# A selective scan on one core: where its decays, its step sizes and its carried state are issued

## The chip, the cores and the metric

The kernel runs on one core of a Trainium2 chip. The metric is the device time of one execution in microseconds. A run gives one such time; the kernel before was timed in three runs, and one further execution was recorded by the profiler.

## What is computed

The program is a network of four layers, each an attention-like part and a feed-forward part with a layer norm behind each, on x of shape (2, 1024, 1024) in float32. The change touches one part alone, the selective scan of the third layer. Cut to what matters, with batch b, channel d of 2048, state n of 16 and time l of 1024 (written here as 1024 steps for each of two sequences):

```python
dt = softplus(einsum('blr,dr->bdl', dt_r, dt_proj_w) + dt_bias)
A = -exp(A_log)                                  # (2048, 16)
def step(h, inp):
    x_t, dt_t, B_t, C_t = inp
    dA  = exp(dt_t[..., None] * A)               # decay
    dBx = dt_t[..., None] * B_t[:, None, :] * x_t[..., None]
    h = dA * h + dBx                             # state, (batch, 2048, 16)
    y = einsum('bdn,bn->bd', h, C_t)
    return h, y
y = (ys + D_param * xc) * silu(z)
out = einsum('bdl,hd->blh', y, out_proj_w)
```

Every other layer is as before.

## The kernel before

The two sequences are worked one after the other (b = 0, 1), and within a sequence the 1024 steps are two halves of 512 (u = 0, 1). In a half, the 2048 channels are 16 chunks (c) of 128, and a chunk is eight **slots**. Slot k of a sequence (0 to 255, the second half from 128 on) handles 16 channels with their 16 states: two tiles (m = 0, 1) of 128 rows, a row being one channel and one state, by 512 steps.

For a slot, `rows` (line 1269) loads dt*x of the slot's channels from DRAM (`dxd`), copied to all 16 states, into a tile h; `times_b` (1278) multiplies it by B on GpSimd; `decay` (1283) spreads dt over the rows with a matmul into PSUM (line 1286) and takes Exp of it times A on ScalarE (1288); `scan` (1293) runs the recurrence on VectorE with one instruction over the 512 steps (1296), decay from PSUM, dt*x*B from h; `times_c` (1306) multiplies by C on VectorE; `states` (1311) sums over the states with matmuls (1318) into y's PSUM tile, every second slot. The tile h has nine buffers.

In the first half a scan starts from 0.0, and `keep` (1300) copies the last column of h to `hst` on ScalarE. In the second half `decay` has one operation more (line 1291): on ScalarE it adds decay times the kept state to the first column of h, and the scan again starts from 0.0.

The step size dt of a chunk comes from `l2_dt` (1208), called 16 slots before the chunk's first slot. It issues a matmul and hangs a chain of small operations of 128x512 on later slots: ScalarE's Relu, Abs, Exp (`act1`), add one, Ln, subtract one (`act2`), then GpSimd's sums (`pool1`, `sum1`), the product with x (`times_x`, 1237, followed by four DMAs that write dxd), and the split of dt into two parts for the decay's matmul (`parts` on ScalarE, `rest` on GpSimd, `send` with two DMAs). x itself is loaded into `xi` by a DMA. The tiles e, one, lg and rl of the chain have one buffer each, and `y_out` (1328) takes the tile "one" as well: it copies y out of PSUM on ScalarE, multiplies by silu(z) on GpSimd and writes it to DRAM.

The order is written out by hand in one loop over k (1479 to 1529). Each engine runs its instructions in the order in which this loop issues them, and waits for semaphores of the others. `at(k, f)` puts f into the list `late[k]`; these run in the middle of slot k, between its two scans. A slot also issues two matmuls (three ahead of slot -1) of other work, taken from a list `todo`: the z projection and the second half's x projection, or the output projection of the first half; their results are copied, convolved or passed through Silu by further `late` operations. All PSUM tiles come from one pool of 8 banks. All DMAs named here go through SyncE's queue (SP), in order.

Of the kernel before, what the change touches and what calls it, by code (L numbers as in the profile page):

```python
# [11 lines left out]
AF = mybir.ActivationFunctionType  # L12
ALU = mybir.AluOpType
# [14 lines left out]
class Net:  # L28
# [1032 lines left out]
    def l2_attn(self, b, ready, last):  # L1061
        nc, i = self.nc, self.i
        NCH, N, NR = 16, 16, 64
        NF = NR + 2 * N
        SL = 8 * NCH
        with (
# [24 lines left out]
            hst = lp.tile([P, NCH * N], F, name=self.nm("hst"))  # L1091

            def tmp(tag, bufs=2, n=HALF):
                return tp.tile([P, n], F, tag=tag, bufs=bufs, name=self.nm(tag))
# [4 lines left out]
            xcd, yd = [dram(t, [P, HALF]) for t in ("xcd", "yd")]  # L1099
# [3 lines left out]
            px, norms, hl, hs, dA, py, xs = {}, {}, {}, {}, {}, {}, {}  # L1103
# [6 lines left out]
            def at(k, f, *args):  # L1110
                late.setdefault(k, []).append((f, args))
# [96 lines left out]
            def l2_dt(u, c, k):  # L1208

                p = self.ps()  # L1210
                nc.tensor.matmul(
                    p, wd[c // 8][: NF + 1, (c % 8) * P : (c % 8 + 1) * P], norms[u][0], start=True, stop=True
                )
                xs[u, c] = xc = tmp("xi")
                at(k + 3, nc.sync.dma_start, xc, xcd[u][c][:])
                e, one, lg = tmp("e", 1), tmp("one", 1), tmp("lg", 1)
                dt, dtx = lg, e
                rl = tmp("rl", 1)

                def act1():  # L1220
                    nc.scalar.activation(rl, p, AF.Relu)
                    nc.scalar.activation(e, p, AF.Abs)
                    nc.scalar.activation(e, e, AF.Exp, scale=-1.0)

                def act2():
                    nc.scalar.activation(one, e, AF.Identity, bias=self.one)
                    nc.scalar.activation(lg, one, AF.Ln)
                    nc.scalar.activation(one, one, AF.Identity, bias=neg)

                def pool1():  # L1230
                    nc.gpsimd.tensor_tensor(e, e, one, ALU.subtract)
                    nc.gpsimd.tensor_tensor(lg, lg, e, ALU.add)

                def sum1():
                    nc.gpsimd.tensor_tensor(dt, lg, rl, ALU.add)

                def times_x():
                    nc.gpsimd.tensor_tensor(dtx, dt, xc, ALU.mult)
                    for j in range(4):
                        nc.sync.dma_start(dxd[u][c][:, j, :], dtx[32 * j : 32 * j + 32, :])  # L1240

                low = [None]

                def parts():

                    hl[u, c] = tp.tile([P, 2, HALF], R, tag="hl", bufs=2, name=self.nm("hl"))
                    nc.scalar.copy(hl[u, c], dt.unsqueeze(1).to_broadcast([P, 2, HALF]))

                def rest():

                    lo = low[0] = tp.tile([P, HALF], R, tag="lo", bufs=1, name=self.nm("lo"))
                    nc.gpsimd.tensor_tensor(lo, dt, hl[u, c][:, 0, :].bitcast(F), ALU.subtract)

                def send():

                    lo = low[0]
                    for j in range(2):
                        nc.sync.dma_start(
                            hl[u, c][64 - 64 * j : P - 64 * j, j, :].bitcast(F), lo[64 * j : 64 * j + 64, :].bitcast(F)
                        )  # L1260

                for n, f in ((1, act1), (2, act2), (3, pool1), (4, sum1), (5, times_x), (7, parts), (7, rest), (8, send)):
                    at(k + n, f)


# [17 lines left out]
            def decay(k, m):  # L1283
                u, c, q, jj = of(k)
                dA[k, m] = self.ps()
                nc.tensor.matmul(dA[k, m], rep[:, 4 * m + q, :], hl[u, c][:, jj, :], start=True, stop=True)  # L1286
                g = 16 * c + 4 * q + 2 * jj + m
                nc.scalar.activation(dA[k, m], dA[k, m], AF.Exp, scale=A[:, g : g + 1])  # L1288
                if u:
                    h0 = hs[k][:, m, 0:1]  # L1290
                    nc.scalar.activation(h0, dA[k, m][:, 0:1], AF.Identity, scale=hst[:, g : g + 1], bias=h0)  # L1291

            def scan(k, m):
                u, c, q, jj = of(k)
                g = 16 * c + 4 * q + 2 * jj + m
                nc.vector.tensor_tensor_scan(  # L1296
                    hs[k][:, m, :], dA.pop((k, m)), hs[k][:, m, :], 0.0, ALU.mult, ALU.add
                )

            def keep(k):  # L1300
# [27 lines left out]
            def y_out(k):  # L1328
                u, c = k // SL, k % SL // 8
                sz = zt.pop((u, c))  # L1330
                yo = tmp("one", 1)
                nc.scalar.copy(yo, py.pop((u, c)))
                nc.gpsimd.tensor_tensor(sz, sz, yo, ALU.mult)
                nc.sync.dma_start(yd[u][c][:], sz)
# [127 lines left out]
            with self.tc.manual_schedule():  # L1462

                todo, ahead = [], []

                def take(units, lead):
                    for n, (load, calls) in enumerate(units):
                        ahead.append((len(todo) - lead, load))
                        todo.extend(calls)

                z0, z1, x1 = gates(0), gates(1), ins(1)
                take(z0[:2] + x1[:6], 20)
                for n in range(2, 12, 2):
                    take(z0[n : n + 2] + x1[n + 4 : n + 6], 20)
                take(xproj(1), 4)
                take(z0[12:] + z1[:6], 20)
                taken = 0
                at(-BEFORE, lambda: at(4 - BEFORE, l2_spread, 0, l2_norm(0)))
                for k in range(-BEFORE, 2 * SL + 6):
                    if -16 <= k < 2 * SL - 16 and k % 8 == 0:  # L1480
                        l2_dt((k + 16) // SL, (k + 16) % SL // 8, k)
                    if k == SL + 12:
                        o = outs(0)
                        for n, (a, z) in enumerate(((6, 10), (10, 12), (12, 16), (16, 16))):
                            take(o[8 * n : 8 * n + 8], 8)
                            take(z1[a:z], 20)
                    if k == -1 or k == SL:
                        l2_cr(max(k, 0) // SL)
                    n = 3 if k < -1 else 2
                    batch = []  # L1490
                    for _ in range(n):
                        while ahead and ahead[0][0] <= taken:
                            ahead.pop(0)[1]()
                        if taken < len(todo):
                            batch.append(todo[taken])
                            taken += 1

                    def pe(last=False):
                        while batch and (last or len(batch) > n - 1):
                            f, *args = batch.pop(0)  # L1500
                            if f:
                                f(*args, k)

                    live = 0 <= k < 2 * SL
                    if 0 <= k + 6 < 2 * SL:
                        rows(k + 6)
                    if 0 <= k + 2 < 2 * SL:
                        times_b(k + 2)
                    if 0 <= k - 1 < 2 * SL:
                        keep(k - 1)  # L1510
                    pe()
                    for m in range(2):
                        if live:
                            scan(k, m)
                        if 0 <= k + 1 < 2 * SL:
                            decay(k + 1, m)
                        if m:
                            break
                        for f, args in late.pop(k, []):
                            f(*args)  # L1520
                        pe(True)
                    if k % 2 == 1 and 0 <= k - 2 < 2 * SL:
                        states(k - 2)
                    if 0 <= k - 1 < 2 * SL:
                        times_c(k - 1)
                    if live and k % 8 == 4:
                        at(k + 8, y_out, k)
                    if live and k % 8 == 0:
                        skip(k // SL, k % SL // 8)
                while late:  # L1530
                    for f, args in late.pop(min(late)):
                        f(*args)
# [460 lines left out]
```

## Time and profile before

| | us |
|---|---|
| median of three runs | 5127.48 (5123.48 to 5133.85) |
| the profiled execution, its own time | 5130.32 |
| its span in the profile | 5128.4 |
| scans of sequence 0, first and second half | 484.4 and 467.0 |
| scans of sequence 1, first and second half | 482.3 and 461.3 |

Mean granted clock of TensorE in the span: 0.968.

How to read it: the profile gives, for each group of instructions, the line, the engine (PE is TensorE, PEld its weight loads, DVE VectorE, ACT ScalarE, POOL GpSimd, SP SyncE), the operation, output<-inputs by tile names and shape, and the count; then the busy time and the mean nanoseconds of one; then the engine's idle time just before them, and what ended it. A line of waits gives who waited for what, the total, how often, and the longest. A line by stage gives the stretch, its length, then busy time and count of PE, PEld, DVE, ACT and POOL. A line of the timeline gives start, length, engine, line and tiles; neighbours of one kind are merged (x2).

### The profile page before, as it was taken

The page shows a single profiled execution, that of the slowest core. Times are in us where ns is not written, and L with a number is a line of the kernel's source. Part 1 is how long each engine was busy: PE and PEld are TensorE (multiplying, and loading weights), DVE is VectorE, ACT ScalarE, POOL GpSimd, SP SyncE. Part 2 cuts the span into 40 slices and gives each one's busy share as a digit, 9 for nine tenths or more (in the row PEclk, how much of TensorE's full clock was granted, in tenths as well). Part 3 has the DMA queues.
Part 4 walks back from the last instruction along what each step waited for, and adds up shares of the span by engine and source line. Part 5 has one row for each costly group of instructions (what it writes and reads, how often), then busy time and mean ns, then how long its engine had stood idle before and what let it go on. Part 6 is the DMA issues. An engine that isn't in the chain of part 4 may idle for free. (4 is left out here: it accounts for less than half of the span.)

```text
span 5128.4 us, 50257 instructions
## 1 busy us (share of the span) xinstructions
PE 4706.3 (92%) x16584; PEld 2237.2 (44%) x16584; DVE 3128.0 (61%) x4322; ACT 2109.7 (41%) x4485; POOL 2097.7 (41%) x1259
## 2 busy tenths in 40 slices
PE   8989989998897888999999999899888988899999
PEld 3347645433332333455433576554333333344544
DVE  5453256389999997225365422652899999963153
ACT  2431232377677774001024311424776777720010
POOL 2013121078798885100020220200887998831010
PEclk9999999999999999999999999999999999999999
DMA  2144212388889998201111432113888899971100
GB/s 88 36 159 143 97 48 81 131 216 217 220 225 242 236 244 226 90 33 46 49 67 38 173 119 89 54 51 103 220 219 224 214 247 245 249 210 65 55 20 33
DMA packets 254871, 708.06 MB, mean 138 GB/s; under 512 B 37008, under 2 KB 54544, under 8 KB 254612
## 3 DMA queue, kind: packets, MB, share of 16 engines
q1 hardware_dynamic: 248340, 683.88, 46.7%
q0 software_dynamic: 6272, 20.98, 1.2%
q8 instruction: 133, 2.18, 0.2%
q14 instruction: 126, 1.03, 0.1%
HBM read 599.60 MB, written 86.25 MB: 134 GB/s over the span
## 5 line engine op out<-in xcount | busy, mean ns | idle before, releaser
L1296 DVE TENSOR_TENSOR_SCAN h<-ps,h 128x512 f32<-128x512 f32 x1024 | 1204.1, 1207 | 88.9 <-ACT h L1291 47.2
L1279 POOL TENSOR_TENSOR h<-h,br 128x1024 f32<-128x1024 f32 x512 | 1201.0, 2367 | 43.3 <-DMA h<-dxd 20.7
L1286 PE MATMUL ps<-hl,rep 128*128 128x512 f32 x1024 | 717.9, 708 | 119.9 <-DVE h L1296 94.7
L1288 ACT ACTIVATE ps<-ps,l_Alog 128x512 f32<-128x512 f32 x1024 | 667.9, 657 | 216.9 <-PE ps L1286 213.6
L1307 DVE TENSOR_TENSOR h<-h,ps 128x1024 f32<-128x1024 f32 x512 | 610.8, 1193 | 0.0
L1403 PE MATMUL ps<-xT,w 128*128 128x512 f32 x1024 | 541.1, 615 | 10.2 <-DVE h L1296 7.9
L1608 POOL TENSOR_TENSOR x<-x,row 128x1024 f32<-128x1024 f32 x48 | 112.3, 2349 | 796.0 <-PE ps L130 796.0
L1286 PEld LDWEIGHTS ps<-hl,rep 128*128 128x128 f32 x1024 | 198.6, 195 | 523.6 <-DVE h L1296 340.1
L152 DVE TENSOR_TENSOR x<-x,ps 128x512 f32<-128x512 f32 x192 | 128.4, 681 | 434.4 <-PE ps L1785 145.6
L1318 PE MATMUL ps<-h,sel 128*32 128x512 f32 x2048 | 365.1, 638 | 18.8 <-DVE h L1307 18.2
L104 PE MATMUL ps<-xT,w 128*128 128x512 f32 x768 | 336.1, 592 | 0.0
L177 ACT ACTIVATE rs<-mv 128x1 f32<-128x1 f32 (+2 forms) x88 | 17.9, 203 | 705.7 <-DVE mv L171 705.4
L1441 PE MATMUL ps<-w,w 128*128 128x512 f32 x512 | 279.9, 630 | 20.8 <-DMA w<-yd 12.1
L1403 PEld LDWEIGHTS ps<-xT,w 128*128 128x128 f32 x1024 | 190.6, 195 | 204.2 <-issue 136.7
L104 PE MATMUL ps<-w,xT 128*128 128x512 f32 (+1 forms) x768 | 278.3, 522 | 0.0
L1124 DVE SCALAR_TENSOR_TENSOR ps<-xp,l_convw,ps 128x512 f32<-128x512 f32 x192 | 144.4, 752 | 213.4 <-ACT ps L1119 208.9
L767 POOL TENSOR_TENSOR s<-s,l1r 128x512 f32<-128x512 f32 x64 | 66.5, 1040 | 487.7 <-DVE l1r L766 481.8
L1349 PE MATMUL ps<-xT,w 128*128 128x512 f32 x512 | 251.9, 602 | 0.7
L1291 ACT ACTIVATE h<-ps,h,hst 128x1 f32<-128x1 f32 x512 | 180.0, 352 | 118.5 <-POOL h L1279 93.9
L1782 PE MATMUL ps<-w,xT 128*128 128x512 f32 x512 | 227.4, 597 | 0.0
L1622 PE MATMUL ps<-w,w 128*128 128x512 f32 x512 | 222.6, 594 | 4.2 <-DMA w<-yd 4.2
L104 PEld LDWEIGHTS ps<-xT,w 128*128 128x128 f32 x768 | 144.8, 189 | 183.4 <-issue 177.6
(289 smaller groups left out, 7319.9 us busy)
## 6 DMA issues: line engine op xcount, KB each, us to landing
h<-dxd SPq DMA_DIRECT2D x512, 512.0 KB, 7.2
w<-l_in SPq DMA_DIRECT2D x128, 512.0 KB, 6.7
w<-l_out SPq DMA_DIRECT2D x96, 512.0 KB, 6.2
w<-l_conv SPq DMA_DIRECT2D x54, 512.0 KB, 3.9
w<-cvd SPq DMA_DIRECT2D x36, 512.0 KB, 3.3
w<-l_fw SPq DMA_DIRECT2D x32, 512.0 KB, 4.4
xcd<-xo SPq DMA_DIRECT2D x64, 256.0 KB, 2.2
xi<-xcd SPq DMA_DIRECT2D x64, 256.0 KB, 5.4
```

What stands on the lines that cost most here:

```text
L104: self.nc.tensor.matmul(out, lhsT, rhs, start=j == 0, stop=j == n - 1)
L1279: nc.gpsimd.tensor_tensor(hs[k], hs[k], norms[of(k)[0]][1].unsqueeze(1).to_broadcast([P, 2, HALF]), ALU.mult)
L1286: nc.tensor.matmul(dA[k, m], rep[:, 4 * m + q, :], hl[u, c][:, jj, :], start=True, stop=True)
L1288: nc.scalar.activation(dA[k, m], dA[k, m], AF.Exp, scale=A[:, g : g + 1])
L1296: nc.vector.tensor_tensor_scan(hs[k][:, m, :], dA.pop((k, m)), hs[k][:, m, :], 0.0, ALU.mult, ALU.add)
L1307: nc.vector.tensor_tensor(hs[k], hs[k], norms[of(k)[0]][3].unsqueeze(1).to_broadcast([P, 2, HALF]), ALU.mult)
L1318: nc.tensor.matmul(py[u, c][32 * j : 32 * j + 32, :], self.sel[:, q, :], hs[k - 1 + j // 2][:, j % 2, :], start=False, stop=q == 3,)
L1349: nc.tensor.matmul(p, w["w"][:, k * P : (k + 1) * P], self.xcols(k, u0, HALF), start=k == 0, stop=k == KD - 1)
L1403: nc.tensor.matmul(p, w["w"][:, k * P : (k + 1) * P], self.xcols(k, u * HALF, HALF), start=k == 0, stop=k == KD - 1)
L1441: nc.tensor.matmul(p, y[:, cc, t * P : (t + 1) * P], wt[:, cc * HALF : (cc + 1) * HALF], start=c2 == 0 and cc == 0, stop=last,)
L1622: nc.tensor.matmul(acc[tt], y[:, cc * HALF + tt * P : cc * HALF + (tt + 1) * P], w[:, cc * HALF : (cc + 1) * HALF], start=c == 0, stop=c = ...
L1782: nc.tensor.matmul(p, self.xcols(k, tt * P, P), wt[k][:, ns], start=k == 0, stop=False)
```

## The change

1. `decay` is issued half a slot sooner. In the middle of slot k stands decay (k+1, 1) where (k+1, 0) stood, and at its end (k+2, 0) where (k+1, 1) stood.
2. dt's chain is spread: `act1` to `act5`, `pool1`, `pool2`, `sum1`, `times_x`, `parts`, `rest` and `send` stand at slots 1, 2, 3, 4, 5, 5, 6, 7, 8, 8, 9 and 10 after `l2_dt`; before, they stood at 1, 2, 3, 4, 5, 7, 7 and 8 with up to three operations together. The load of xi moves from slot 3 to slot 4, and dt*x goes to the tile "one", not e.
3. In the second half the scan takes its first state straight from the column of `hst` in SBUF, and line 1291 is gone.
4. `y_out` copies y into a tile of its own, "yo".

```diff
-                at(k + 3, nc.sync.dma_start, xc, xcd[u][c][:])
+                at(k + 4, nc.sync.dma_start, xc, xcd[u][c][:])
                 e, one, lg = tmp("e", 1), tmp("one", 1), tmp("lg", 1)
-                dt, dtx = lg, e
+                dt, dtx = lg, one
                 rl = tmp("rl", 1)
 
                 def act1():
                     nc.scalar.activation(rl, p, AF.Relu)
                     nc.scalar.activation(e, p, AF.Abs)
+
+                def act2():
                     nc.scalar.activation(e, e, AF.Exp, scale=-1.0)
 
-                def act2():
+                def act3():
                     nc.scalar.activation(one, e, AF.Identity, bias=self.one)
+
+                def act4():
                     nc.scalar.activation(lg, one, AF.Ln)
+
+                def act5():
                     nc.scalar.activation(one, one, AF.Identity, bias=neg)
 
                 def pool1():
                     nc.gpsimd.tensor_tensor(e, e, one, ALU.subtract)
+
+                def pool2():
                     nc.gpsimd.tensor_tensor(lg, lg, e, ALU.add)
...
-                for n, f in ((1, act1), (2, act2), (3, pool1), (4, sum1), (5, times_x), (7, parts), (7, rest), (8, send)):
+                for n, f in (
+                    (1, act1), (2, act2), (3, act3), (4, act4), (5, act5), (5, pool1), (6, pool2), (7, sum1),
+                    (8, times_x), (8, parts), (9, rest), (10, send),
+                ):
                     at(k + n, f)
...
                 nc.scalar.activation(dA[k, m], dA[k, m], AF.Exp, scale=A[:, g : g + 1])
-                if u:
-                    h0 = hs[k][:, m, 0:1]
-                    nc.scalar.activation(h0, dA[k, m][:, 0:1], AF.Identity, scale=hst[:, g : g + 1], bias=h0)
...
                 nc.vector.tensor_tensor_scan(
-                    hs[k][:, m, :], dA.pop((k, m)), hs[k][:, m, :], 0.0, ALU.mult, ALU.add
+                    hs[k][:, m, :], dA.pop((k, m)), hs[k][:, m, :], hst[:, g : g + 1] if u else 0.0, ALU.mult, ALU.add
                 )
...
-                yo = tmp("one", 1)
+                yo = tmp("yo", 1)
...
-                        if 0 <= k + 1 < 2 * SL:
-                            decay(k + 1, m)
+                        if 0 <= k + 1 + m < 2 * SL:
+                            decay(k + 1 + m, 1 - m)
```

## The prediction

> **What bounds the kernel now.** I read the page's groups first, then cut the four scan stages (two sequences, two halves each, from the first scan of each to the first of the next) out of the trace and asked for busy time in each, then for who waited for whom there. Busy time by stage (PE, PEld, DVE, ACT, POOL; then clock, DMA share, GB/s):
>
> ```profile
> 1052.00:1536.40 484.40, 428.78 (x1341) 162.80 (x1339) 462.92 (x438) 345.03 (x659) 418.91 (x226) 0.97 0.84 220
> 1536.40:2003.40 467.00, 395.33 (x1241) 147.64 (x1239) 440.18 (x398) 339.46 (x674) 399.58 (x212) 0.95 0.93 240
> 3601.90:4084.20 482.30, 429.11 (x1342) 163.08 (x1340) 463.09 (x437) 344.90 (x659) 419.04 (x226) 0.97 0.83 220
> 4084.20:4545.50 461.30, 395.99 (x1240) 146.71 (x1238) 439.69 (x398) 339.56 (x674) 399.70 (x212) 0.95 0.93 244
> ```
>
> The four take 1895.0 us of the span's 5128.4. VectorE is busy for 1805.9 of them, 95%, so it sets their length, and 1895.0 - 1805.9 = 89 us is all that better timing can win. Outside these stages the change touches nothing. Where the 89 us are (from the page):
>
> ```profile
> L1296 DVE TENSOR_TENSOR_SCAN h<-ps,h 128x512 f32<-128x512 f32 x1024 | 1204.1, 1207 | 88.9 <-ACT h L1291 47.2
> ...
> L1291 ACT ACTIVATE h<-ps,h,hst 128x1 f32<-128x1 f32 x512 | 180.0, 352 | 118.5 <-POOL h L1279 93.9
> ```
>
> The scans alone wait 88.9 us: 47.2 for line 1291, ScalarE's one-column operation of the second halves. The list of waits gives the rest for a first half (ended by the decay's Exp, line 1288) and shows that a second half has no other wait:
>
> ```profile
> DVE h L1296 <- ACT ps L1288: 13.2, 14, 2.3
> DVE h L1296 <- DMA dxd<-e: 5.7, 1, 5.7
> ...
> DVE h L1296 <- ACT h L1291: 26.1, 33, 2.3
> ```
>
> 5.7 us in each sequence is the wait before its very first scan, which stays. So 88.9 - 11.4 = 77.5 us of waits are open to the change. A typical one, on ScalarE's timeline (second half, slot 168; the second scan of slot 169 started at 1685.78 after a wait of 1.62 us):
>
> ```profile
> 1680.94 1.28 ACT L1388 ACT_TABLE_LOAD   x1
> 1682.24 1.15 ACT L1388 ACTIVATE zo<-zo 128x512 f32<-128x512 f32 x2
> 1683.41 1.28 ACT L193 ACT_TABLE_LOAD   x1
> 1684.70 0.66 ACT L1288 ACTIVATE ps<-ps,l_Alog 128x512 f32<-128x512 f32 x1
> 1685.40 0.35 ACT L1291 ACTIVATE h<-ps,h,hst 128x1 f32<-128x1 f32 x1
> ```
>
> The decay's matmul was done 5.0 us before the scan. Its Exp sat behind a block of other ScalarE work queued in the same slot, and line 1291 behind the Exp. Most waits look like this; eight, before the first scan of a chunk, end with line 1291 waiting for GpSimd's times_b.
>
> **Decays half a slot sooner.** No instruction more or less. In a slot ScalarE now runs Exp (k+1,1), the block, Exp (k+2,0), in place of (k+1,0), block, (k+1,1): what follows the block is due one scan and one times_c later. By the busy rows those take about 1.12 + 1.11 = 2.2 us back to back (a pair of scans shows as 2.33 us, a times_c as 1.19 with some 0.08 overlapped). The largest ScalarE wait in steady state is 2.3 us, most are under 1.7: nearly all are covered. The price is a third decay tile alive in PSUM. Counting lifetimes by hand (one bank for C, one or two for y, one or two for the running products, one for dt's product), at most 7 of 8 banks were taken in program order and now 8. PE waits already, 435 us in all at the decays' weight loads, for a scan to free a bank, mostly the third or fourth before its own; the third leaves 3.4 us for the matmul (0.8) and Exp (0.66), enough. PE has 1895.0 - 1649.2 = 246 us free to hide this; without that cover each wait would come back at the scan.
>
> **State from SBUF.** It removes 512 operations of 352 ns, 180 us of ScalarE, all beside VectorE's work except the last 0.35 us before a scan that waits; and ScalarE no longer waits 93.9 us for times_b. It adds a per-partition operand in SBUF to 512 scans, which are on the path. No scan of before has one; the nearest rows, all 512 columns with a PSUM input:
>
> ```profile
> L1124 DVE SCALAR_TENSOR_TENSOR ps<-xp,l_convw,ps 128x512 f32<-128x512 f32 x192 | 144.4, 752 | 213.4 <-ACT ps L1119 208.9
> L152 DVE TENSOR_TENSOR x<-x,ps 128x512 f32<-128x512 f32 x192 | 128.4, 681 | 434.4 <-PE ps L1785 145.6 <-PE ps L104 144.3 <-PE ps L1622 100.5
> ...
> L1723 DVE SCALAR_TENSOR_TENSOR x<-ps,rinv,x 128x512 f32<-128x512 f32 x32 | 22.9, 746 | 9.0 <-PE ps L104 8.7 <-issue 0.3
> ```
>
> Lines 1124 and 1723 have such an operand, 152 has none: 746 ns against 681 (687 at the median): 59 to 65 ns. Pairs agree: two of L1723 span 1.41 us, two of L152 1.26 to 1.28. A gain is excluded (nothing is taken out of the scan); the bounds are 0[...] and 71 ns (start to start, 665 against 594). I take 59: 512 x 59 ns = **30.2 us added**, in second halves only. These scans now wait for GpSimd's times_b themselves, beside the Exp; behind a waiting scan stand the next scan and times_c, as in the first halves, where such waits come to 2.1 us.
>
> Here a rule speaks against the change. The Trainium skill ("SBUF — State Buffer", section "SBUF: two separate sides") says that a VectorE instruction with two SBUF inputs and a GpSimd instruction exclude each other for their whole length. The trace agrees for two SBUF tensors: line 181 on 12 columns takes 2.26 us exactly while a times_b runs.
>
> ```profile
> 1386.44 4.63 POOL L1279 TENSOR_TENSOR h<-h,br 128x1024 f32<-128x1024 f32 x2
> ...
> 1386.54 2.26 DVE L181 TENSOR_TENSOR rsq<-rsq,ss 128x12 f32<-128x12 f32 x1
> ```
>
> If the state counted as a second SBUF input, a scan would find GpSimd busy with chance 399.6/467.0 = 0.86 and wait half a 2.37 us operation: about 1.0 us x 512 = 520 us. But line 1124 has just the new scan's mix (one PSUM and one SBUF tensor, an SBUF scalar) and runs in the first halves beside GpSimd busy 86%: longest 758 ns of 192. So the sum goes by the row, 30.2 us.
>
> **dt's chain, one operation a slot.** Same operations, 64 chunks. On ScalarE the bursts of three (0.59 + 0.60 + 0.63 and 0.71 + 0.63 + 0.72) become two and single ones; on GpSimd two bursts (2 x 1.27 in one slot; dt's sum beside y's product in the next) become one 1.27 us operation a slot, 2.37 + 1.27 = 3.64 us, about a slot's 3.6 to 3.8. times_x waited 15.2 us for xi in a second half: xi is now loaded one slot later but used four slots after, and it goes past y's store, which waits on GpSimd (up to 7.1 us on SP), so that wait should go. The four dxd writes move three slots later (10.9 us), the two hl writes two (7.3). From issue and landing records: dxd lands 3.1 us (median) after times_x, and is followed 5.6 us later by the chunk's first read of it. Less 10.9, plus about 2.7 of burst that no longer precedes times_x, rows will wait some 2.6 us on SP. Behind it stand the next rows (which wait for an h buffer anyway), hl's writes and weights loaded 8 to 20 products ahead. h now lands 8.8 us before its times_b (least 4.3), hl 13.5 us before its decay (least 7.0): medians stay positive, the worst chunks touch zero. pool1 now waits for act5 of its own slot; behind it stands the times_b of a scan two slots (7 us) later. I charge 5 us in all.
>
> **y's copy in its own tile.** It no longer waits for "one" (0.9 us in a second half), and is needed since "one" now holds dtx until its DMA has read it: free by about two slots before act3 rewrites it. Cost nothing; if that margin fails ScalarE waits, covered as above.
>
> **Sum.** Left of the 77.5 us: about 7 (start-up scans and the norm), 8 (GpSimd or DMA late in second halves), 5 (chain edges) = 20. So -57.5 + 30.2 = **-27.3**. The profiled execution ran 5130.3 us, giving 5103; it lies 2.8 above the median of 5127.5, so I forecast **5100** (-0.5%).
>
> **Rivals.** (A) The operand is free: -57.5, **5070**. [...]against: three rows. 13%. (B) Decays sooner in the program but not on the chip: the eighth bank makes PE wait for the same scans, half the waits stay: -38.7 + 30.2 = -8.5, **5119**. For: 434.8 us of waits on scans at decays; against: in the waits shown the matmul was long done. 14%. (C) Slower: the later chain. Its place is the first two slots of each chunk: dxd late, rows queued, then hl behind them, PE stuck in order at the decay. At 1 us of VectorE wait per chunk, 64 us: -27 + 64, **5164**. It decides from 27/64 = 0.43 us a chunk. Against: the margins above and the two slots that times_b runs ahead. 12%. (D) The lock: over **5600**, 3%.
>
> **Numbers.** The forecast case has 58%, own range 5085 to 5116. Range 5063 to 5128: A, B and the forecast inside, most of C and D out. About 0.2% (10 us) is what a measurement here can tell from no change. Faster: 0.58 + 0.13 = 0.71; same: B 0.14; slower: 0.15.
>
> **What will show it.** Line 1296's mean: 1207 in first halves, about 1265 in second ones (1207: A; over 2000: D). First halves shorter by 10 us or more each, second halves by about 3, with VectorE busy near 455. Waits of scans under 35 us, ended by GpSimd or Exp. SP's wait of rows on dxd: some 2.6 us a chunk; under C, scans at a chunk's first slot waiting for times_b or Exp with PE stopped by hl's DMA. If the first halves do not shorten, the ordering argument is wrong; if second halves lengthen with scans at 1207, the chain is.

## The result, and the profile after

| | before | after |
|---|---|---|
| median, us | 5130.66 (4 runs) | 5166.94 (4 runs, 5156.38 to 5169.78) |
| the profiled execution, us | 5130.32 | 5156.38 |
| its span, us | 5128.4 | 5154.7 |
| scans, sequence 0, first and second half | 484.4, 467.0 | 508.5, 454.2 |
| scans, sequence 1, first and second half | 482.3, 461.3 | 510.4, 455.8 |

Ratio of after to before 1.0065, 95% interval 1.0046 to 1.0084: slower by 0.65%, where 0.5% faster was forecast. The profiled execution of after is the fastest of its four, so its profile shows rather less than the median's loss: the span grew by 26.3 us, the four stages together by 33.9.

By stage, after (stretch, its length, then PE, PEld, DVE, ACT, POOL busy and counts, clock, DMA share, GB/s):

```profile
1047.10:1555.60 508.50, 423.81 (x1344) 158.10 (x1342) 464.47 (x437) 340.38 (x660) 415.90 (x225) 0.95 0.78 209
1555.60:2009.80 454.20, 390.64 (x1238) 142.95 (x1238) 451.95 (x398) 256.54 (x418) 403.30 (x215) 0.94 0.92 248
3607.20:4117.60 510.40, 429.01 (x1344) 160.30 (x1342) 464.47 (x438) 339.98 (x660) 415.93 (x225) 0.94 0.78 207
4117.60:4573.40 455.80, 391.02 (x1239) 143.36 (x1238) 452.03 (x398) 256.39 (x418) 403.27 (x215) 0.94 0.92 248
```

The second halves are 12.8 and 5.5 us shorter: VectorE is busy for 12 us more in each, and waits for almost nothing. The first halves are 24.1 and 28.1 us longer though VectorE's busy time there rose by only 1.5: the loss is waiting, and it lies in the halves in which neither the scan's instruction nor line 1291 changed. The groups of the page say who waits, first `times_c` in before, then after:

```profile
L1307 DVE TENSOR_TENSOR h<-h,ps 128x1024 f32<-128x1024 f32 x512 | 610.8, 1193 | 0.0
```

```profile
L1299 ACT ACTIVATE ps<-ps,l_Alog 128x512 f32<-128x512 f32 x1024 | 674.8, 663 | 599.4 <-PE ps L1297 597.4
...
L1315 DVE TENSOR_TENSOR h<-h,ps 128x1024 f32<-128x1024 f32 x512 | 611.2, 1194 | 71.3 <-ACT hst L1312 71.3
L1304 DVE TENSOR_TENSOR_SCAN h<-ps,hst,h 128x512 f32<-128x512 f32 x512 | 627.9, 1263 | 5.9 <-POOL h L1290 3.3
L1304 DVE TENSOR_TENSOR_SCAN h<-ps,h 128x512 f32<-128x512 f32 x512 | 599.7, 1207 | 16.7 <-ACT ps L1299 16.7
```

In after, L1297 and L1299 are the decay's matmul and Exp (before, L1286 and L1288), L1304 the scan (L1296), L1315 `times_c` (L1307) and L1312 `keep` (L1304 before). The scans wait for 22.6 us in place of 88.9, as was meant. But `times_c`, which before waited for nothing, now waits 71.3 us for `keep`, whose source h it overwrites, and all of that is in first halves (`keep` does nothing in a second half). VectorE's waits in the first one:

```profile
DVE h L1315 <- ACT hst L1312: 35.4, 12, 4.8
DVE h L1304 <- ACT ps L1299: 7.4, 4, 5.7
```

One of them, on ScalarE's and then VectorE's timeline of after (slot 12; the **block** is the other ScalarE work that `late` puts into the slot, from behind the first Exp to behind the second table load, ACT_TABLE_LOAD):

```profile
1097.02 0.66 ACT L1299 ACTIVATE ps<-ps,l_Alog 128x512 f32<-128x512 f32 x1 [4.82 <-PE ps L1297]
...
1098.74 1.28 ACT L1129 ACT_TABLE_LOAD   x1
...
1101.68 1.28 ACT L193 ACT_TABLE_LOAD   x1
1102.98 0.66 ACT L1299 ACTIVATE ps<-ps,l_Alog 128x512 f32<-128x512 f32 x1
1103.56 0.18 ACT L1312 COPY hst<-h 128x2 f32<-128x2 f32 x1
...
1103.78 1.22 DVE L1315 TENSOR_TENSOR h<-h,ps 128x1024 f32<-128x1024 f32 x1 [4.84 <-ACT hst L1312]
```

The same slot in the kernel before:

```profile
1100.27 0.66 ACT L1288 ACTIVATE ps<-ps,l_Alog 128x512 f32<-128x512 f32 x1 [1.53 <-PE ps L1286]
...
1104.41 1.28 ACT L193 ACT_TABLE_LOAD   x1
1105.70 0.66 ACT L1288 ACTIVATE ps<-ps,l_Alog 128x512 f32<-128x512 f32 x1
1106.29 0.18 ACT L1304 COPY hst<-h 128x2 f32<-128x2 f32 x1
...
1106.40 1.22 DVE L1296 TENSOR_TENSOR_SCAN h<-ps,h 128x512 f32<-128x512 f32 x1 [2.32 <-ACT ps L1288]
```

Before, Exp (13,1) ran behind the block and its scan waited 2.32 us; `keep` (12), right behind it, was in time. After, Exp (13,1) stands ahead of the block and its scan is nearly in time. But for that Exp ScalarE first stands idle for 4.82 us until its matmul is done, so the block, Exp (14,0) and `keep` (12) all come later, and `times_c` (12) pays 4.84.

Why is the matmul late? PE's timeline of before, of after, and of the version below that copies y out sooner, each at the first matmul of a new chunk's y (line 1324, before 1316: D times x, into a fresh PSUM bank):

```profile
1095.17 1.13 PE L1316 MATMUL ps<-xi,dg 128*128 128x512 f32 x2 [1.74 <-DVE h L1296]
```

```profile
1091.98 1.73 PE L1324 MATMUL ps<-xi,dg 128*128 128x512 f32 x2 [2.86 <-DVE h L1304]
...
1096.18 0.80 PE L1297 MATMUL ps<-hl,rep 128*128 128x512 f32 x1
```

```profile
1095.49 1.12 PE L1324 MATMUL ps<-xi,dg 128*128 128x512 f32 x2 [0.66 <-DVE h L1304]
```

By the count of lifetimes eight banks are wanted at that point in after: the old y is copied out only in slot 12, the new y begins at the end of slot 11, and three decays are alive. The new y's first matmul takes the bank of a scan that has only just ended. Which one fits the count: scan (11,1) in after, (11,0) in before and with y copied sooner, where seven are wanted, and in the last experiment, with six, it waits for no scan. Behind this matmul in PE's order stand the sums over the states and the next decays. Against the end of scan (12,1), from the trace's records, in us:

| slot 12 of sequence 0 | before | after | y copied sooner | Exps at the old place |
|---|---|---|---|---|
| y's first matmul starts | -6.66 | -3.30 | -6.66 | -3.31 |
| matmul of decay (13,1) | -0.33 | +0.90 | -3.31 | +0.81 |
| Exp (13,1) | +3.88 | +1.74 | -2.77 | +2.78 |
| block's first table load | -0.37 | +3.46 | -1.54 | -1.46 |
| wait of `times_c` (12) | 0 | 4.84 | 0.14 | 0 |

Slots 28, 44, 60 and 76 of each first half repeat slot 12, with 4.84 us each. `times_c` of slots 16, 32, 48, 64 and 80 waits about 2.1 us each, with a matmul that is no later than before: there the new order alone is at work (in one of the ten, with 2.9 us, the matmul is 0.5 us later too). In sequence 0 the two kinds make up 34.5 of the 35.4 us.

### The profile page after: what moved, and what is told of

Read it like the earlier page. It is cut to its first block, busy times and chain, and to the rows that moved or that the text cites. A ratio compares the mean times of both kernels' runs of the same rounds, so it can differ in the third digit from the quotient of the medians.

```text
span 5154.7 us, 49250 instructions
## 1 busy us (share of the span) xinstructions
PE 4680.2 (91%) x16584; PEld 2213.3 (43%) x16584; DVE 3155.2 (61%) x4322; ACT 1933.6 (38%) x3973; POOL 2094.5 (41%) x1259
## 5 line engine op out<-in xcount | busy, mean ns | idle before, releaser
L1290 POOL TENSOR_TENSOR h<-h,br 128x1024 f32<-128x1024 f32 x512 | 1207.7, 2371 | 31.3 <-DMA h<-dxd 25.5
L1299 ACT ACTIVATE ps<-ps,l_Alog 128x512 f32<-128x512 f32 x1024 | 674.8, 663 | 599.4 <-PE ps L1297 597.4
L1297 PE MATMUL ps<-hl,rep 128*128 128x512 f32 x1024 | 695.7, 685 | 190.4 <-DVE h L1304 154.0
L1315 DVE TENSOR_TENSOR h<-h,ps 128x1024 f32<-128x1024 f32 x512 | 611.2, 1194 | 71.3 <-ACT hst L1312 71.3
L1304 DVE TENSOR_TENSOR_SCAN h<-ps,hst,h 128x512 f32<-128x512 f32 x512 | 627.9, 1263 | 5.9 <-POOL h L1290 3.3
L1304 DVE TENSOR_TENSOR_SCAN h<-ps,h 128x512 f32<-128x512 f32 x512 | 599.7, 1207 | 16.7 <-ACT ps L1299 16.7
L1297 PEld LDWEIGHTS ps<-hl,rep 128*128 128x128 f32 x1024 | 199.8, 197 | 647.6 <-DVE h L1304 469.2
L1326 PE MATMUL ps<-h,sel 128*32 128x512 f32 x2048 | 318.2, 664 | 5.1 <-DVE h L1315 5.0
```

The costliest lines, as they stand in the source:

```text
L1290: nc.gpsimd.tensor_tensor(hs[k], hs[k], norms[of(k)[0]][1].unsqueeze(1).to_broadcast([P, 2, HALF]), ALU.mult)
L1304: nc.vector.tensor_tensor_scan(hs[k][:, m, :], dA.pop((k, m)), hs[k][:, m, :], hst[:, g : g + 1] if u else 0.0, ALU.mult, ALU.add)
L1315: nc.vector.tensor_tensor(hs[k], hs[k], norms[of(k)[0]][3].unsqueeze(1).to_broadcast([P, 2, HALF]), ALU.mult)
L1326: nc.tensor.matmul(py[u, c][32 * j : 32 * j + 32, :], self.sel[:, q, :], hs[k - 1 + j // 2][:, j % 2, :], start=False, stop=q == 3,)
```

## The experiments

The theory from these profiles: the decays' new place is the whole loss, through `keep` (K). The rival is the one that was given 12% ahead (C): dt's later chain. Four kernels separate the parts; all ratios are to the kernel before on the same chip, with 95% intervals, and the lengths of the four stages come from one profiled execution each. Executions of one kernel spread over some 20 us, so stages that differ by less than about 5 us are not told apart. In four kernels (after, the first experiment, "no `keep`" and the last experiment) the profiled execution is the fastest of its kernel, so for totals the ratio counts, not the sum of the stages.

**All of the change but the decays.**

```diff
-                        if 0 <= k + 1 + m < 2 * SL:
-                            decay(k + 1 + m, 1 - m)
+                        if 0 <= k + 1 < 2 * SL:
+                            decay(k + 1, m)
```

> The changed kernel with one part undone: decays stand at their old places, dt's chain, the state from SBUF and yo stay. Theory K (with decays sooner, the decay (k+1,1)'s Exp stands ahead of the slot's block of other ScalarE work and waits for PE, the block starts later, and keep, which times_c waits for, stands behind the block): the waits of times_c on keep (71.3 us) go, the waits of scans on Exp come back in part. First halves 475 to 488 us each (508.5 and 510.4 in the changed kernel), second halves 455 to 468; time about 5120 to 5135, level with before. Theory C (the later chain of dt: late dxd and hl): first halves stay over 500, time over 5150.

Measured: 5122.86 us, ratio 0.9989 (0.9982 to 0.9995); stages 481.0, 458.6, 479.2 and 457.7. With the decays back in place the loss is gone, so C falls.

**The decays alone**, the kernel before with only the opposite of that edit.

> The kernel before with decays half a slot sooner and nothing else. Theory K: times_c waits for keep also here, a little less than in the changed kernel since the block lacks act4 and parts (0.64 and 1.04 us): first halves 492 to 508 us, second halves no longer than 467 and 461; time 5135 to 5160. Theory C: without the later chain nothing is lost, first halves at or under 484, time at or under 5130.

Measured: 5194.80, ratio 1.0119 (1.0103 to 1.0135); stages 509.4, 466.2, 507.5 and 470.6. The sign and the first halves are as K has them (`times_c` waits 30.0 and 29.0 us for `keep`), but the time lies well above the 5135 to 5160 that were expected. With line 1291 still there the second halves gain nothing either: their scans wait 23.4 and 28.2 us for it, where it was 26.1 and 21.1. The other parts of the change were hiding some of the loss.

**The state from SBUF alone.**

```diff
-                if u:
-                    h0 = hs[k][:, m, 0:1]
-                    nc.scalar.activation(h0, dA[k, m][:, 0:1], AF.Identity, scale=hst[:, g : g + 1], bias=h0)
...
-                    hs[k][:, m, :], dA.pop((k, m)), hs[k][:, m, :], 0.0, ALU.mult, ALU.add
+                    hs[k][:, m, :], dA.pop((k, m)), hs[k][:, m, :], hst[:, g : g + 1] if u else 0.0, ALU.mult, ALU.add
```

> The kernel before with the state read from SBUF by the scans of the second half, line 1291 gone, nothing else. First halves unchanged (484 and 482). A scan of a second half takes 1263 in place of 1207 ns: 28.7 us added in all; the waits for line 1291 (47.4 us) go, and some come back as waits for Exp and times_b. If 20 us come back: 5130 + 28.7 - 47.4 + 20 = 5131; if none, 5111. If the waits were PE's or GpSimd's own lateness all come back: 5155.

Measured: 5123.06, ratio 0.9990 (0.9983 to 0.9998); stages 483.1, 457.4, 482.6 and 457.2. In the second halves this takes away line 1291's 47.2 us of waits, adds 24 to VectorE's busy time and leaves 10.1 of new waits, mostly for GpSimd: -13, and the two stages are 13.7 shorter.

**The chain alone**: parts 2 and 4 of the change, with decays and line 1291 as before.

> The kernel before with dt's chain one operation a slot, xi loaded a slot later, dtx in the tile one and y's copy in yo; decays and line 1291 as before. Theory K: harmless or a small gain; 5115 to 5135, first halves 475 to 488. Theory C: the loss is here: over 5150, with scans of a chunk's first slot waiting.

Measured: 5111.28, ratio 0.9961 (0.9946 to 0.9976); stages 484.2, 462.0, 481.4 and 451.5. What had been charged 5 us is the best single part, worth 0.4%: in the second halves line 1291's waits fall to 23.7 and 14.4 us. It and the state do not add: all but the decays (0.9989) is slower than the chain alone. The second halves show a part of the reason. With the chain spread, the state from SBUF has 38.1 us of line 1291's waits to take away, not 47.2; it leaves 11.3 us of waits for the Exp, and VectorE is busy 29.1 us longer (904.4 against 875.3 us). So there it costs 2 to 3 us where alone it gained 13. The rest of the difference does not show in the two profiled executions.

The second question is how `keep` comes to be late. Either the copy itself is in the way (K1), or the block is late and `keep` is only first in line behind it (K2). And if it is the block: is PE late for want of a bank (P), or is it the order on ScalarE, an Exp that waits put ahead of the block (O)?

**No `keep`.** This kernel leaves the copy of the last column out and holds zeros in `hst`, so the second half starts from a zero state and not from the first half's.

```diff
-                    nc.scalar.copy(hst[:, g : g + 2], hs[k][:, :, HALF - 1])
...
+            nc.gpsimd.memset(hst, 0.0)
```

> The changed kernel with keep left out (hst is set to zero once, so the second half starts from a zero state and the output is not the reference's). Theory K1 (keep's place behind the block is the whole cause): the 71.3 us of times_c's waits are simply gone, first halves about 473 us, time about 5095. Theory K2 (the block of ScalarE work itself starts too late, since the decay's Exp ahead of it waits for PE; keep is only the first thing behind it that VectorE meets): the Exp (k+2,0) behind the same block is needed one scan pair later, so at slots 12, 28, ... about 3.5 of the 4.8 us come back as waits of scans for Exp, at slots 16, 32, ... about 0.5 of 2.1; first halves about 490 to 497, time about 5130 to 5140.

Measured: 5141.82, ratio 1.0041 (1.0026 to 1.0057); stages 493.0, 457.3, 493.3 and 455.4. The wait moves one row on, to the next scan, (14,0): the profile names no releaser for it ("issue"), but its Exp, behind the late block, ends just before it starts. ScalarE and VectorE at slot 12 of this kernel (its L1300 is the Exp, L1305 the scan):

```profile
1098.99 0.66 ACT L1300 ACTIVATE ps<-ps,l_Alog 128x512 f32<-128x512 f32 x1 [6.25 <-PE ps L1298]
...
1104.95 1.24 ACT L1300 ACTIVATE ps<-ps,l_Alog 128x512 f32<-128x512 f32 x2
...
1105.70 2.34 DVE L1305 TENSOR_TENSOR_SCAN h<-ps,h 128x512 f32<-128x512 f32 x2 [3.68 <-issue]
```

K2 holds: the block is late, and without `keep` the first halves still lose some 10 us.

**Decays sooner in the second halves only** (in the first, the old order).

```diff
-                        if 0 <= k + 1 + m < 2 * SL:
-                            decay(k + 1 + m, 1 - m)
+                        j = (k + 1 + m, 1 - m) if k >= SL else (k + 1, m)
+                        if k == SL - 1 and m:
+                            decay(k + 1, m)
+                            j = (k + 2, 0)
+                        if 0 <= j[0] < 2 * SL:
+                            decay(*j)
```

> The changed kernel with decays sooner in the second halves alone. Both forms of theory K lie in the first halves (keep exists there alone): first halves as with decays back (481 and 479), second halves as in the changed kernel (454 and 456): about 7 us under the kernel with decays back, 5110 to 5118, and faster than before. If the loss also sat in the handing over between slots whatever keep does, second halves would stay at 458 and the time at 5123.

Measured: 5122.66, ratio 0.9993 (0.9984 to 1.0002); stages 479.4, 456.8, 479.8 and 456.9. The first halves recover as in the first experiment, but the second ones are no better than with the decays at the old place (458.6, 457.7): the expected gain there did not show. Once the state comes from SBUF, hardly a wait is left in them to take (11.3 us in the two with the decays back).

**y copied out two slots sooner**, so that at most seven banks are wanted; all else as in after.

```diff
-                        at(k + 8, y_out, k)
+                        at(k + 6, y_out, k)
```

> The changed kernel with y's copy out of PSUM two slots sooner (at(k + 6)), so that the old y bank is free before the next chunk's y takes one and at most 7 banks are taken as before. Theory P (the eighth bank: the skip matmul at a chunk's start waits up to 3.2 us for a scan to free a bank, the decay behind it is late, ScalarE's Exp (k+1,1) waits for it and the block behind starts late): these waits go, the block at slots 12, 28, ... starts about 3 us sooner, times_c's waits fall from 71 to under 30 us, first halves 480 to 490, time 5115 to 5130. Theory O (the order on ScalarE alone, banks or not): only the copy's 0.58 us leave the block, first halves 500 to 506, time 5150 to 5162.

Measured: 5116.43, ratio 0.9984 (0.9974 to 0.9993); stages 484.4, 454.5, 486.7 and 452.2. One number undoes the loss, as theory P has it. Its waits of `times_c` in the first half, in place of after's 35.4 us:

```profile
DVE h L1315 <- ACT hst L1312: 14.2, 6, 3.5
```

At slot 12 the wait falls from 4.84 to 0.14 (table above). What is left are slots such as 16 and 32: there the matmul of decay (17,1) runs 1.06 us before the reference scan's end in before, in after and here alike, but since its Exp now stands ahead of the block, the block's first table load comes at +1.4 in place of -2.1, and `times_c` waits 2.35 us where it waited for nothing.

**The matmuls sooner, the Exps at the old place**: three decays alive in PSUM as in after, ScalarE's order as before.

```diff
-            def decay(k, m):
+            def spread(k, m):
...
+            def decay(k, m):
...
-                            decay(k + 1 + m, 1 - m)
+                            spread(k + 1 + m, 1 - m)
+                        if 0 <= k + 1 < 2 * SL:
+                            decay(k + 1, m)
```

> The changed kernel with the decays' matmuls half a slot sooner on PE but their Exps at the old places on ScalarE: three decay tiles stay alive in PSUM, and the block stands ahead of Exp (k+1,1) again. Theory O (order on ScalarE): first halves back at 484 or under, waits of times_c on keep gone, time 5110 to 5130. Theory P (banks): first halves stay over 500, time over 5150.

Measured: 5123.12, ratio 0.9996 (0.9987 to 1.0005); stages 480.3, 457.7, 477.7 and 462.4. VectorE's first entry in the first half's waits is a scan again, and `times_c` is not among them:

```profile
DVE h L1307 <- ACT ps L1302: 16.0, 8, 5.7
```

PE is as late as in after (last column of the table above), and the total does not rise. So P and O are both right and neither is enough for the whole loss: the eighth bank makes the matmul late, and the new order hands that lateness to the block. A lower clock is not the cause: in after's first halves the granted clock was 0.95 and 0.94, where before had 0.97 twice, but this version had 0.95 in both and lost nothing.

The third question: does a version beat both kernels?

**Second halves' decays sooner, and y copied sooner.** The edits of "decays sooner in the second halves only" and of "y copied out two slots sooner" together.

> The changed kernel with decays sooner in the second halves alone and y's copy two slots sooner. If the two findings add up (order on ScalarE: first halves want the old one, 479 us; banks: second halves 452 to 454 with the y bank free), the four stages come to about 1866 us against 1895 of the kernel before: 5100 to 5110. If y's sooner copy only paid by mending the order's loss, second halves stay at 456 and the time at 5115 to 5123.

Measured: 5112.79, ratio 0.9966 (0.9954 to 0.9978); stages 475.5, 458.7, 477.1 and 454.6. The stages sum to the 1866 us that were expected, but the time falls between the two cases. Its first halves have the old order of decays, those of "y copied out two slots sooner" the new one (484.4 and 486.7), both with banks free: so the new order costs some 9 us in each even then. The second halves are those of that version too, 458.7 and 454.6 where it had 454.5 and 452.2: so far apart can two executions lie.

**The same with line 1291 in place of the state from SBUF**, at the place where the decays stood before.

```diff
+            def start(k, m):
...
+                    nc.scalar.activation(h0, dA[k, m][:, 0:1], AF.Identity, scale=hst[:, g : g + 1], bias=h0)
...
-                    hs[k][:, m, :], dA.pop((k, m)), hs[k][:, m, :], hst[:, g : g + 1] if u else 0.0, ALU.mult, ALU.add
+                    hs[k][:, m, :], dA.pop((k, m)), hs[k][:, m, :], 0.0, ALU.mult, ALU.add
...
+                        if 0 <= k + 1 < 2 * SL:
+                            start(k + 1, m)
```

> The same with line 1291 in place of the state from SBUF, at its old place (half a slot after its decay's Exp). The 56 ns that the SBUF operand adds to each of 512 scans (28.7 us measured) go; the waits of scans for line 1291 return. If decays sooner cover the Exp, 5 to 12 us of waits per second half: 445 to 450 each, time 5085 to 5100, under the kernel with the SBUF operand. If line 1291's own place behind the block is what the scans waited for, 20 to 26 us return per half: 458 to 464, time 5115 to 5130.

Measured: 5113.62, ratio 0.9966 (0.9952 to 0.9980); stages 479.3, 458.4, 477.4 and 467.0. Of the expectation's two cases the second came, that line 1291's place behind the block is what the scans wait for. VectorE is busy for 439.0 and 439.2 us in the second halves in place of 451.8 and 451.6, and waits 19.0 and 27.5 us for line 1291: in this order the two ways of starting a scan cannot be told apart.

**The chain, and y copied sooner**: decays and line 1291 as before.

> The kernel before with dt's chain one operation a slot, yo, and y's copy two slots sooner; decays and line 1291 as before, so at most 6 banks are taken. Theory P says that the old order had banks to spare and loses nothing by them: within 5 us of the chain alone (5111). If banks limited the kernel before as well, first halves fall from 484 and 481 by 5 us or more each and the time under 5105.

Measured: **5100.37**, ratio 0.9946 (0.9933 to 0.9960): faster than both kernels. By stage:

```profile
1049.80:1528.40 478.60, 430.90 (x1341) 161.75 (x1339) 462.48 (x437) 337.06 (x659) 417.33 (x226) 0.98 0.84 221
1528.40:1976.40 448.00, 397.96 (x1243) 147.00 (x1242) 436.82 (x398) 339.09 (x674) 401.38 (x214) 0.96 0.94 256
3575.70:4051.60 475.90, 430.03 (x1342) 161.46 (x1340) 463.27 (x438) 337.16 (x658) 417.22 (x226) 0.98 0.83 222
4051.60:4501.70 450.10, 396.03 (x1241) 146.77 (x1240) 436.98 (x398) 339.17 (x674) 401.24 (x214) 0.96 0.95 255
```

Against the chain alone the first halves fall by 5.6 and 5.5 us, the second case of the expectation. With two decays alive, y's first matmul waited there too, 11.8 us in PE's weight loads of a first half, and now 1.5; the matmul of decay (13,1) moves from -1.53 to -3.30 on the scale of the table, the block from -1.04 to -1.95, and the wait of scan (13,1) falls from 1.65 to 0.74 us (at (29,1), (45,1), (61,1) and (77,1), in both sequences, from 1.64 or more to 0.73 to 0.75). So the early copy takes some waits away by itself. That it makes the whole faster than the chain alone is not shown: the two intervals (0.9933 to 0.9960 and 0.9946 to 0.9976) overlap. That it is the bank and not the copy's new place among ScalarE's work was not separated either.

Against the version just above, the second halves are shorter, 448.0 and 450.1 in place of 458.4 and 467.0: there the decays' matmuls and Exps were sooner, and line 1291 made the scans wait 46.5 us in place of 24.2. So where line 1291 stays, the decays' new place did not pay in the second halves either, as with the decays alone. This kernel with the state from SBUF as well was not run.

## Why the prediction was wrong

**What bounds the kernel**: right. VectorE sets the stages' lengths before and after.

**Decays half a slot sooner**: this step failed. It said "what follows the block is due one scan and one times_c later" and "nearly all are covered", and looked only at the scans. Two things were left out. First, `keep` also stands behind the block, and `times_c` waits for it: 71.3 us, where the step counted no new wait. Second, the block does not stay where it is. An Exp that is put ahead of it brings its own wait for PE along. ScalarE's waits at the decays in the first half of sequence 0, before and after:

```profile
ACT ps L1288 <- PE ps L1286: 43.5, 57, 4.0
```

```profile
ACT ps L1299 <- PE ps L1297: 112.2, 88, 6.0
```

With all of the change but the decays' new place they are 23.5 us, so the rise is this step's; the block starts 3.8 us later at slot 12. Taken alone the step lost 1.19%, and against the rest of the change it makes the difference between 0.9989 and 1.0065.

**Its price in PSUM**: the count of eight banks was right; "246 us free to hide this" was the wrong measure. Free time on average says nothing of the one place in a chunk where PE stops in order, with the decays queued behind. The step did say that without this cover a wait would come back at the scan; it came back at `times_c`. That the third scan before "leaves 3.4 us" for matmul and Exp, "enough", holds for the scan and fails for the block. Rival B named the bank, but priced it as waits that stay (5119) and not as waits that grow; no case ended near 5167 by this way. C did (5164), by a mechanism that the first experiment refutes: its number is luck.

**The state from SBUF**: right. 1263 ns against 1207 in the same execution is 56, forecast 59. (The forecast took the lower end of its rows: line 1124's own mean is 752 ns, not 746, 71 over line 152's.) From the start of a scan to the start of the next one right behind it the median is 1133 ns without the operand and 1194 with it, 61. In sum it is a little less: VectorE's busy time in the second halves rose by 11.8 and 12.3 us, 24.1 / 512 = 47 ns a scan, for the 30.2 us charged. Line 1291's waits are gone, and GpSimd's `times_b` makes scans wait for 3.3 us in all. A is refuted by the operand's cost, D by these 1263 ns with GpSimd busy for 403 of 454 us: the rule of the Trainium skill ("SBUF — State Buffer", section "SBUF: two separate sides") does not reach a one-column operand beside one tensor in SBUF, as the row of line 1124 had said.

**dt's chain**: wrong in sign. The waits on SP were smaller than forecast (in sequence 0 rows wait 13.8 us for dxd in the first half and 12.4 in the second, 0.9 and 0.8 us a chunk, forecast 2.6), and hardly a scan waits behind them. Parts 2 and 4 gave 0.39% by themselves, line 1291's shorter waits among it; which of their pieces gains the rest was not separated.

**y's copy in its own tile**: "free by about two slots" was too much: ScalarE waited 36.3 us for dxd's write to free "one", 15 times. It was also so with the decays back (21.9 us), without harm to be seen. What mattered was not the tile but when y is copied.

**The sum**: forecast -27.3, the profiled execution shows +26. Second halves -18.3 (forecast about -6), first halves +52.2 (forecast at least -20): 71.3 us of new waits of `times_c`, less 14.7 us by which the scans' waits for the Exp fell (31.3 to 16.6).

## What to carry to other kernels

Before an instruction is put ahead of a block on an in-order engine, ask what it waits for: its wait becomes the block's, and everything that stands behind the block has to be looked up, small copies that guard a buffer too. A pool of buffers that a change fills to the last one costs at the place where two long lives overlap, and there the lateness goes to whatever is queued in order behind; shortening one of those lives can take the loss away (here, copying y out two slots sooner: 1.0065 to 0.9984). Parts that each take the same waits don't add, so each is best run alone.

## What the runs showed of the hardware

A per-partition operand in SBUF costs a scan of 512 steps 56 ns in the mean of the record, 47 ns in VectorE's busy time, and 61 ns from start to start of two scans back to back (1133 to 1194). In the profiled executions of the last seven kernels, on other chips than the first four, the means of both kinds of scan are longer (1323 and 1227 ns with y copied sooner and the second halves' decays sooner), while VectorE's busy time in a second half is the same (451.8 and 451.6 us; in after 452.0 in both) and the scans follow one another just as fast (1133 and 1193 ns): the records overlap more there, so the busy time of the stage and the time from start to start are the figures to compare. Executions of one kernel on one chip spread from 5119.91 to 5141.77 us (43 of the kernel before): a single execution cannot show a difference of 0.2%, but the waits inside it can be read one by one.
